# Local transformer inside a twelve-stage network: where the closing part's norm, its last products and the norm's result stand in a four-round schedule

## The chip, the core and the metric

The kernel runs on one core of one Trainium2 chip. The time is device microseconds of that core for one execution of the whole network. Of three runs of the kernel before, the median is 5578.49 us (5568.84 to 5580.77). One more execution was profiled; all views below come from it.

## The reference, cut to what matters

The network has twelve stages, each added to the running `x`. Two of them (seventh and ninth) are the same local transformer, six layers deep:

```python
for i in range(DEPTH):                       # DEPTH = 6
    x = attn_layer(shift_tokens(x), Wqkv[i], q_scale[i], k_scale[i], Wo[i]) + x
    x = ffn_layer(shift_tokens(x), ln_g[i], ln_b[i], W1[i], b1[i], W2[i], b2[i]) + x

def ffn_layer(x, g, bln, W1, b1, W2, b2):
    mu = x.mean(-1, keepdims=True)
    var = ((x - mu) ** 2).mean(-1, keepdims=True)
    xn = (x - mu) / jnp.sqrt(var + 1e-05) * g + bln
    a, gate = jnp.split(xn @ W1 + b1, 2, -1)
    return a * jax.nn.gelu(gate, approximate=False) @ W2 + b2
```

`attn_layer` has 16 heads of 64: projections, an l2 norm of q and k, a rotation of both, softmax over windows of 32 queries by 64 keys, weighted values, and the product with `Wo`. Everything is float32.

## The kernel before, in words

Features lie on the partitions, tokens along the free dimension. The 2048 tokens are four groups of 512. In a local stage, one layer of one group is a *unit*: 24 units per stage, 48 in the whole program. A unit's 16 heads are done four at a time, as four *quads*, so a stage has 96 quads.

`ffn2` (L1593) is a software pipeline written out by hand. Each pass of its loop is a *round*, in which four quads of different age are served: q0 is projected, q1 gets its scores, q2 its exponentials, transposes and weighted values, q3 its context turned back. The order of statements is the order in which each engine gets its work: `_Ordered` (L285) chains every engine's instructions, so none of the engines reorders them. In a steady round TensorE (PE) does this, with the tiles' names as the profile shows them: `bank<-sb_cs,l_rn` (quad_pick, L1361: 16 tiny matmuls; its start is used below as the start of a round), `pp` (quad_project, for k and then for q), `et` (quad_turn: transposes of the exponentials), `bank<-l_sq` (quad_norms), `ct` (quad_back), `cx` (quad_weigh: 128 small matmuls of 64x32 weights, in two halves of 64), `sc` (quad_scores: a mask, then 128 small matmuls), `vp` (quad_values). ScalarE (ACT) squares `pp` into `l_sq`, takes the exponential `l_e`, copies `et` out as `l_at` (which `cx` reads) and `ct` out as `l_ct`, does two steps for the roots (`lv`, `l_rn`) and copies `vp` out as `l_v`. VectorE (DVE) does `l_rq`, two shuffles, the scaled keys `l_kp`, then the start of the rotation (`l_yk`, a shuffle `l_yr`, `l_yq`, a second shuffle `l_yr`), then `l_rc` and `l_cx` for each half of `cx`, then `l_mx` and `l_e` from `sc`. GpSimd (POOL) finishes the rotation in four operations and scales `l_e`.

The large PSUM tiles (`pp`, `et`, `ct`, both halves of `cx`, `sc`, `vp`, `ge`) share three pairs of banks (`two`, L1294). Which pair each of them gets is settled when the program is built, so a reordering can give other instructions each other's buffers. Two more banks hold `bank` and `acc`.

The rest of a unit, its closing part, is the generator `local_rest` (L1472). `ffn2` advances it by one step at four places of each round: A after the q projection and before the transposes (L1620), B after the weighted values and before the scores (L1632), C right behind B (L1633), D after the values (L1638). So it runs over four rounds, sixteen places:

- first round, *output round*: three groups of products with `Wo` (`wo_acc`) at A, B and D; at D also x1 (the residual add) and its shifted copy.
- second, *norm round*: at A the norm's mean (a matmul with a constant matrix, in the profile `acc<-l_xs`), `ln_c` = x minus mean on DVE, its square `ln_sq` on ACT; nothing at B and C; at D the variance (`acc<-ln_sq`), Ln and Exp on ACT (`lv`, `ln_r`), and on DVE the result `t` = `ln_c` times `ln_r`, and then times gamma plus beta.
- third, *gelu round*: at C two of three `ge` pairs (products with W1, Gelu on ACT, `l_ag` on DVE), with a table load on ACT ahead; at D the third pair, a table load back, and the first two products with W2 (`second(0)` and `second(1)`, in the profile `w_acc`).
- fourth, *last round*: at A the third product and x2 (the residual add).

Where a step yields False at B or D, a piece of a background queue (the next stage's norms) is pumped; a step that yields True keeps it away. `settle` (L482) lets an unfinished background piece run to its end first, because the norm's working tiles (`scratch`, L405) are shared with it.

Of the kernel before, what the change touches and what calls it, by code (L numbers as in the profile page):

```python
# [23 lines left out]
AF = mybir.ActivationFunctionType  # L24
ALU = mybir.AluOpType
# [14 lines left out]
INNER = 341  # L40
# [268 lines left out]
class _Net:  # L309
# [1162 lines left out]
    def local_rest(self, u):  # L1472


        nc, i = self.nc, u.i
        acc = self.bank1("wo_acc")

        def project(cs):
            for c in cs:
                self.mm(acc, u.w["wo"][:, c, :], u.ct[c // 2][:, c % 2, :], start=c == 0, stop=c == 7)  # L1480

        project(range(3))
        yield False
        project(range(3, 6))
        yield False
        yield False
        project(range(6, 8))
        u.x1 = self.new_x()
        nc.vector.tensor_tensor(u.x1, acc, self.ys[u.g], ALU.add)
        xs = self.shifted(u.x1)  # L1490
        yield False

        self.settle()
        norm = self.norm_parts(xs, gamma=self.get(f"F{i}_ln_g"), beta=self.get(f"F{i}_ln_b"),
                               out=self.scratch("t", bufs=2), bank=self.bank1)
        next(norm)
        yield True
        yield True
        yield True
        u.hn = yield from norm  # L1500
        yield False

        yield False
        yield False
        o = self.bank1("w2_acc")
        ags = []

        def second(m):
            f = GE_CHUNKS[m][1]
            self.mm(o, u.w["w2"][:f, m, :], ags[m][:f, :], start=m == 0, stop=m == 2)  # L1510

        def first(m):
            f, w = GE_CHUNKS[m]
            pp = self.two("ge")
            self.mm(pp[:w, 0, :], u.w["w1"][:, INNER + f : INNER + f + w], u.hn)
            self.mm(pp[:w, 1, :], u.w["w1"][:, f : f + w], u.hn)
            gl = self.work("l_gl", bufs=2)
            self.act(gl[:w, :], pp[:w, 0, :], AF.Gelu, bias=self.get(f"F{i}_b1", 3 + m, 1)[:w, :])
            ag = self.work("l_ag", bufs=2)
            nc.vector.scalar_tensor_tensor(ag[:w, :], pp[:w, 1, :],  # L1520
                                           self.get(f"F{i}_b1", m, 1)[:w, :], gl[:w, :],
                                           ALU.add, ALU.mult)
            ags.append(ag)

        self.table("gelu_and_others")
        first(0)
        first(1)
        yield True
        first(2)
        self.table(LN_EXP)  # L1530
        second(0)
        second(1)
        yield False

        second(2)
        x2 = self.new_x()
        nc.vector.scalar_tensor_tensor(x2, o, self.get(f"F{i}_b2"), u.x1, ALU.add, ALU.add)
        self.ys[u.g] = x2
        if i == DEPTH - 1:
            z = self.new_x()  # L1540
            nc.vector.scalar_tensor_tensor(z, x2, 0.5, self.x[u.g], ALU.mult, ALU.add)
            self.finish(u.g, z)
        yield False
# [235 lines left out]
```

## Time and profile before

| what | value |
|---|---|
| median of three runs | 5578.49 us |
| the profiled execution | 5561.13 us, span 5559.4 us |
| PE busy | 5031.0 us (90%) |
| DVE, ACT, POOL busy | 3494.9, 2440.1, 2344.1 us |
| mean granted TensorE clock | 0.962 |
| norm matmuls, first to last start | 1089.5 to 4882.2 us |
| matmuls of the scores, first to last start | 985.3 to 4859.1 us |

Between the two local stages, from about 2800 to 3050 us, another stage runs. In the four views of the prediction's sample unit, times are microseconds from the start of the span. A timeline row gives start, duration, engine, operation, output<-inputs, count, and in brackets the idle time of the engine just before it with what ended it; "issue" there means that no semaphore did. L300 is the line of a recording helper and says nothing. Matmul ends are modelled, so distances from start to start are safer than durations.

### The profile page before, as it was taken

How to read it: one execution, taken by the hardware profiler on the slowest of the kernel's cores; microseconds unless marked ns; L12 is line 12 of the kernel's file. 1: busy time of each engine (PE TensorE's matmuls, PEld its weight loads, DVE VectorE, ACT ScalarE, POOL GpSimd, SP SyncE). 2: the span in 40 equal slices, each digit the busy share in tenths (PEclk: the TensorE clock that was granted, in tenths of full speed). 3: DMA queues.
4: the chain of work that ended last, by engine and by line, in shares of the span. 5: the costliest groups of instructions: out<-in, count | busy, mean ns of one | idle time of the engine just before them, and what ended most of it. 6: DMA issues, size and time to landing. Idle time of an engine off the chain costs nothing.

```text
span 5559.4 us, 161655 instructions
## 1 busy us (share of the span) xinstructions
PE 5031.0 (90%) x73456; PEld 3009.9 (54%) x73456; DVE 3494.9 (63%) x5863; ACT 2440.1 (44%) x2947; POOL 2344.1 (42%) x1205
## 2 busy tenths in 40 slices
PE   9999997899899899988889899989998988899889
PEld 6755754455555555555544455555555555555446
DVE  4444446767767767776645676767767676645555
ACT  2233235444545444444434444545444444433442
POOL 0000022666666666666500666666666666501000
PEclk9999999999999999999989999999999999999999
DMA  1000000111111111111000011111111111000000
GB/s 67 1 1 1 1 1 23 30 35 39 35 40 33 39 34 42 34 35 34 26 23 1 27 38 37 36 40 33 39 34 42 34 35 35 27 34 1 1 1 8
DMA packets 58334, 149.55 MB, mean 27 GB/s; under 512 B 9649, under 2 KB 23858, under 8 KB 57394
## 3 DMA queue, kind: packets, MB, share of 16 engines
q1 hardware_dynamic: 57650, 139.21, 8.3%
q8 instruction: 578, 9.47, 0.7%
q14 instruction: 106, 0.87, 0.1%
HBM read 45.52 MB, written 1.05 MB: 8 GB/s over the span
## 4 chain that ended last, share of the span: by engine, by line
PE 72%; DVE 17%; ACT 6%; issue 4%; POOL 1%; DMA 0%; SPq 0%; DVEq 0%; ACTq 0%; POOLq 0%
PE mm L355 10%; PE pp L300 10%; PE sc L300 7%; PE vp L300 7%; PE e_o L355 6%; PE wo_acc L300 6%; PE bank L300 6%; PE ge L300 5%; DVE l_yr L300 5%; PE cx L300 4%; PE ms L300 3%; PE w_acc L300 2%; DVE l_yk L300 2%; DVE l_yq L300 2%; PE ct L300 2%
## 5 line engine op out<-in xcount | busy, mean ns | idle before, releaser
L300 POOL TENSOR_TENSOR l_yr<-l_yr,l_ksin 128x1024 f32<-128x1024 f32 x192 | 456.8, 2379 | 1024.0 <-DVE l_yr L300 1024.0
L300 PE MATMUL pp<-l_xs,wqkv 128*128 128x512 f32 x1536 | 718.6, 611 | 5.3 <-DMA wqkv<-in_f_wqkv 3.7
L300 ACT COPY l_v<-vp 128x1024 f32<-128x1024 f32 x192 | 194.4, 1013 | 859.3 <-PE vp L300 859.3
L300 ACT ACTIVATE l_sq<-pp 128x1024 f32<-128x1024 f32 x384 | 391.4, 1019 | 283.3 <-PE pp L300 283.3
L300 DVE STREAM_SHUFFLE l_yr<-pp 128x1024 f32<-128x1024 f32 x384 | 505.9, 1318 | 0.0
L300 POOL TENSOR_TENSOR l_e<-l_e,l_rq 128x1024 f32<-128x1024 f32 x192 | 365.7, 1905 | 331.1 <-DVE l_e L300 301.4
L355 PE MATMUL mm<-x,m 128*128 128x512 f32 x1024 | 475.4, 604 | 1.4 <-ACT e_a L387 1.4
L300 DVE TENSOR_REDUCE l_mx<-sc 128x16 f32<-128x1024 f32 x192 | 235.1, 1224 | 374.6 <-PE sc L300 374.6
L300 POOL TENSOR_TENSOR l_yq<-l_yq,l_yr 128x1024 f32<-128x1024 f32 x192 | 456.0, 2375 | 15.0
L300 POOL TENSOR_TENSOR l_yk<-l_yk,l_yr 128x1024 f32<-128x1024 f32 x192 | 453.1, 2360 | 15.1
L300 POOL TENSOR_TENSOR l_yr<-l_yr,l_qsin 128x1024 f32<-128x1024 f32 x192 | 455.1, 2370 | 0.0
L300 PE MATMUL cx<-l_w,l_at 64*32 64x65 f32 x12288 | 304.0, 235 | 148.7 <-ACT l_at L300 123.2
L300 PEld LDWEIGHTS pp<-l_xs,wqkv 128*128 128x128 f32 x1536 | 279.1, 192 | 291.6 <-issue 285.8
L300 PE MATMUL sc<-l_kp,l_yq 64*32 64x64 f32 x24576 | 326.2, 236 | 104.1 <-issue 103.2
L300 PE MATMUL vp<-wqkv,l_xs 128*128 128x256 f32 x1536 | 399.5, 404 | 6.5 <-issue 5.3
L355 PEld LDWEIGHTS e_o<-m,e_h 128*128 128x128 f32 x3072 | 362.9, 192 | 60.6 <-issue 60.1
L300 PEld LDWEIGHTS sc<-l_kp,l_yq 64*32 64x32 f32 x24576 | 277.5, 111 | 172.0 <-issue 170.8
L300 PEld LDWEIGHTS cx<-l_w,l_at 64*32 64x32 f32 x12288 | 261.5, 109 | 197.7 <-ACT l_at L300 137.5
L355 PE MATMUL e_o<-m,e_h 128*128 128x128 f32 x3072 | 363.5, 275 | 0.0
L300 PE MATMUL wo_acc<-l_ct,wo 128*128 128x512 f32 x768 | 358.0, 599 | 0.1
L300 PEld LDWEIGHTS vp<-wqkv,l_xs 128*128 128x128 f32 x1536 | 286.3, 196 | 61.0 <-issue 10.5
L300 PE MATMUL cx<-l_v,l_at 64*32 64x65 f32 x12288 | 309.3, 236 | 6.0 <-issue 6.0
(285 smaller groups left out, 9513.1 us busy)
## 6 DMA issues: line engine op xcount, KB each, us to landing
l_w<-l_v SPq DMA_DIRECT2D x192, 390.0 KB
wqkv<-in_f_wqkv SPq DMA_DIRECT2D x48, 384.0 KB
l_w<-l_v SPq DMA_DIRECT2D x192, 65.0 KB
wo<-in_f_wo SPq DMA_DIRECT2D x12, 512.0 KB
l_rt<-l_rn SPq DMA_DIRECT2D x384, 8.0 KB
m<-in_m_w SPq DMA_DIRECT2D x16, 256.0 KB
w<-in_f_w SPq DMA_DIRECT2D x12, 341.0 KB
w<-in_f_w SPq DMA_DIRECT2D x12, 192.0 KB
```

The lines of the kernel that those rows point to most:

```text
L300: r = f(*args, **kw)
L355: self.nc.tensor.matmul(out, lhsT=lhsT, rhs=rhs, start=start, stop=stop)
```

## The change

Only `local_rest` changes, and all of it is a matter of place. The mean, `l_lc` (formerly `ln_c`) and the square move from A to B of the norm round. The variance, Ln and Exp stay at D. The two DVE operations that make the norm's result move from D of the norm round to A of the gelu round. `second(1)` moves from D of the gelu round, and `second(2)` with x2 from A of the last round, both to B of the last round. The centred x and the reciprocal root get tiles of their own (`l_lc`, `l_lr`). The places that pump the background queue are the same as before.

```diff
         xs = self.shifted(u.x1)
         yield False
 
+        yield False
         self.settle()
-        norm = self.norm_parts(xs, gamma=self.get(f"F{i}_ln_g"), beta=self.get(f"F{i}_ln_b"),
-                               out=self.scratch("t", bufs=2), bank=self.bank1)
-        next(norm)
+        xc, r = self.work("l_lc"), self.work("l_lr")
+        m = self.bank1("mean")
+        self.mm(m, self.get("mean"), xs)
+        nc.vector.tensor_tensor(xc, xs, m, ALU.subtract)
+        sq = self.scratch("ln_sq")
+        nc.scalar.activation(sq, xc, AF.Square)
         yield True
         yield True
-        yield True
-        u.hn = yield from norm
+        v = self.bank1("var")
+        self.mm(v, self.get("mean"), sq)
+        self.rsqrt(r, v, 0)
         yield False
 
+        hn = self.scratch("t", bufs=2)
+        nc.vector.tensor_tensor(hn, xc, r, ALU.mult)
+        nc.vector.tensor_scalar(hn, hn, self.get(f"F{i}_ln_g"), self.get(f"F{i}_ln_b"), ALU.mult,
+                                ALU.add)
         yield False
         yield False
         o = self.bank1("w2_acc")
...
         first(2)
         self.table(LN_EXP)
         second(0)
+        yield False
+
+        yield False
         second(1)
-        yield False
-
         second(2)
         x2 = self.new_x()
         nc.vector.scalar_tensor_tensor(x2, o, self.get(f"F{i}_b2"), u.x1, ALU.add, ALU.add)
```

In the built program the PSUM pairs of three of the four rounds are dealt out differently: in the norm round and the last round the second half of `cx` takes the pair of `ct` and so waits for ACT's `l_ct`; in the gelu round it takes the pair of the q projection and waits for DVE's second `l_yr`.

More of the change, by code (lines that the diff above doesn't have):

```diff
@@ L1514, in first @@
             pp = self.two("ge")
-            self.mm(pp[:w, 0, :], u.w["w1"][:, INNER + f : INNER + f + w], u.hn)
-            self.mm(pp[:w, 1, :], u.w["w1"][:, f : f + w], u.hn)
+            self.mm(pp[:w, 0, :], u.w["w1"][:, INNER + f : INNER + f + w], hn)
+            self.mm(pp[:w, 1, :], u.w["w1"][:, f : f + w], hn)
             gl = self.work("l_gl", bufs=2)
```

## The prediction

> **What bounds the kernel.** First the page's engine shares, then the longest waits of PE.
>
> ```profile
> PE 5031.0 (90%) x73456; PEld 3009.9 (54%) x73456; DVE 3494.9 (63%) x5863; ACT 2440.1 (44%) x2947; POOL 2344.1 (42%) x1205
> ```
>
> ```profile
> PE cx L300 <- ACT l_at L300: 123.2, 48, 3.3
> PE sc L300 <- issue: 103.2, 87, 2.0
> ...
> PE ge L300 <- DVE l_yr L300: 27.1, 43, 0.9
> ```
>
> PE is the bound; whatever shortens its queue in a round shortens the round. Of its idle time in the local stages, two entries stand out, and each comes about once per unit: 48 waits of `cx` for `l_at` (there are 48 units), and 87 waits of `sc` for nothing that has a semaphore. To place them I took one unit and asked for its norm, gelu and last rounds (they start at 1463.54, 1481.84 and 1503.03; the next round starts at 1517.81). On PE:
>
> ```profile
> 1474.17 0.25 PE L300 MATMUL cx<-l_w,l_at 64*32 64x65 f32 x2 [2.62 <-ACT l_at L300]
> ...
> 1478.04 1.09 PE L300 MATMUL sc<-l_kp,l_yq 64*32 64x64 f32 x88 [1.47 <-issue]
> ...
> 1486.45 1.09 PE L300 MATMUL et<-sb_c,l_e 128*128 128x128 f32 x8 [0.34 <-ACT l_e L300]
> ...
> 1492.31 3.70 PE L300 MATMUL ge<-t,w 128*128 128x512 f32 x8 [0.60 <-DVE l_yr L300]
> ...
> 1514.75 1.20 PE L300 MATMUL sc<-l_kp,l_yq 64*32 64x64 f32 x100 [1.59 <-issue]
> ```
>
> The first wait is the norm round's. Why `l_at` is late stands in ACT's queue:
>
> ```profile
> 1472.59 0.63 ACT L300 ACTIVATE ln_sq<-ln_c 128x512 f32<-128x512 f32 x1 [3.45 <-DVE ln_c L300]
> 1473.12 0.99 ACT L300 COPY l_at<-et 128x1024 f32<-128x1024 f32 x1
> ```
>
> ACT sat 3.45 us at the head of its queue for `ln_c`, which DVE reaches only behind the whole rotation; the copy that `cx` needs was queued behind it. The gelu round starts with DVE in the same position:
>
> ```profile
> 1483.39 0.85 DVE L300 TENSOR_TENSOR t<-ln_c,ln_r 128x512 f32<-128x512 f32 x1 [1.74 <-ACT ln_r L300]
> 1484.28 0.55 DVE L300 TENSOR_SCALAR t<-t,sb_pv 128x512 f32<-128x512 f32 x1
> 1484.74 0.17 DVE L300 TENSOR_SCALAR l_rq<-bank 128x16 f32<-128x16 f32 x1
> ```
>
> DVE waits 1.74 us for `ln_r` with keys and rotation behind it, so `l_rq` is done 3.1 us into the round, against 0.9 in the last round, and `cx` and `ge` are held by `l_yr`. The stretch from one round's start to the next, averaged over the trace: 19.0 us for 46 norm rounds, 21.4 for 44 gelu rounds, 15.3 for 44 last rounds (14.8 typical; four carry background work). Drains hold the others.
>
> **Dense work.** From start to start in rounds without a wait, PE needs: pick 0.57, `pp` 3.54, `et` 0.97, sums 0.99, `ct` 1.03, `cx` 1.42, mask 0.32, `sc` 1.41, `vp` 1.93; together 12.2 us. One 512-column float32 product of the closing part adds 0.86.
>
> **The stall in sc.** The last round holds one product: 12.2 + 0.86 = 13.05, against 14.8 measured, so the stall costs about 1.8 us, more than the 1.59 in the bracket (modelled ends). It comes in norm and last rounds, where `sc` follows `cx` directly; in output and gelu rounds 2.8 or 3.7 us of long matmuls lie between the two and `sc` shows none. Its place moves by some 25 matmuls from unit to unit. The page's queue 8, "instruction", moved 9.47 MB in 578 packets, 16.4 KB each. I read it as code arriving too slowly for 256 small matmuls in a row: 9.47 MB for PE's 146,912 instructions is 64 bytes each, so a block of 16 KB is 128 matmuls with their weight loads, run in 1.45 us, while 1.45 + 1.8 = 3.25 us (an estimate) passes between blocks. The Trainium skill speaks against this: "Runtime: NRT & Kernel Launch", section "Instruction fetch mechanics", gives the 16 KiB blocks of 256 instructions but says that fetching is mostly hidden, since issue is slower than the fill. By that rule a filler between `cx` and `sc` buys nothing; by the row it buys its own length, up to 1.8. I take the row, for the stall is absent just where filler stands, and keep the rule as a rival.
>
> **Norm round.** Removed: the mean ahead of `et`, `ln_sq` ahead of `l_at`. Without filler, `et` waits for the exponential and starts 4.6 into the round (gelu round's row) instead of 4.1 + 0.86. `ct` starts at 6.6, the first half of `cx` at 7.6; `l_at` is ready by then (gelu round: 6.75). The second half now waits for `l_ct`, which ended 2.15 us after `ct` began in the gelu round: 8.8 instead of 8.3, a new wait of 0.45. Its price lies between 0 and the 2.62 of the old wait; I take 0.45 because ACT has nothing ahead of `l_ct` now. `cx` ends at 9.5, the mean takes it to 10.4. The stall of 1.8 is covered by 0.86 and, half the time, by the 0.45: 0.7 is left. `sc` with mask 1.73 + 0.7 gives 12.8, `vp` 14.7, variance 15.6. Against 19.0: 3.4 us less. The old figure includes some 0.6 us of half-speed clock: the granted clock falls to 0.5 in 34 of the 46 norm rounds, behind the idle `cx`.
>
> Free moves: `l_lc` on DVE stands behind `l_cx`, ahead of `l_mx`, where DVE idled 2.33 us for `sc`; `ln_sq` falls into ACT's 4.71 us of idleness before `l_v`. Were that cover gone, each would cost its 0.65 us. Neither SP nor POOL is passed: shifted copy and all DMAs keep their places.
>
> **Gelu round.** Removed: 1.74 us of waiting and 1.4 of work ahead of `l_rq`. DVE then runs as in the last round, where the second `l_yr` ends at 8.67. The norm's result follows, 0.85 + 0.55: done at 10.1. Behind it are queued `l_rc` and `l_cx` (`ge` and the next `ct` wait for them; done 11.75 against 12.05 before) and the first `ge`, which begins at 10.1 instead of 10.66. `cx` is not in the way: its second half waits for `l_yr` to 8.7 and ends at 9.4. From `ge` on 3.63 + 0.32 + 1.42 + 1.83 + 1.72 as before, and one product instead of two, 0.9: 19.95. Bounds for `ge`: 9.4 (`cx`'s end) to 11.9 (no earlier rotation). Gain 1.45.
>
> **Last round.** `et` 4.6; `cx` as in the norm round, to 9.5; two products 1.72 in place of the one ahead of `et`; the stall covered; `sc` 1.73 and `vp` 1.93: 14.9. Before, 14.8 typical: nothing, for the stall pays for the product from the gelu round and the two waits. x2 (0.73) on DVE sits ahead of `l_mx` while PE is still in `sc`. `acc` is held until x2, at about 12, and next needed 7 us later. Bounds 14.4 to 16.7 (stall unchanged).
>
> **Output round.** No change; its exponential needs POOL's `l_e`, which ended 2.97 into it, 0.5 ahead of need. After: rotation 6.3 + 4 x 2.37, then 1.9, less 14.9: 2.8.
>
> **Sum.** 46 x 3.4 = 156, 44 x 1.45 = 64, 44 x 0.1 = -4: 216 us. The profiled execution took 5561.1 (span 5559.4 and 1.7 around it): 5345. It lies 17.4 below the median of the runs; the median should go to 5578.5 - 216 = 5362.
>
> **Rivals.** (1) The stall is no matter of filler and keeps its 1.8. Norm rounds gain 2.3 (106), gelu rounds 64, last rounds lose 1.9 (82): 88 less, 5490. For it: the skill's rule, and a single 0.86 product is short. Against: the two kinds of rounds without the stall. (2) The norm's result holds `ge` up: at 11.9 instead of 10.1 the gelu round loses 1.8, 79 in all: 5441. For it: `ge` is now right behind it. Against: the last round shows DVE 1.8 us earlier once nothing stands in front. (3) Slower: dealing the PSUM pairs differently makes a new standing wait. The second half of `cx` waits for `l_ct` or `l_yr` in norm, gelu and last rounds, 134 times. Above 216 / 134 = 1.6 us more each than I counted, the whole is slower; if all were as late as `l_at` was, 2.62, that is 2.17 more, 291 us: 5653. Against: `l_ct` took no longer than 2.15 us after `ct` in a round with a free ACT.
>
> **Numbers.** The forecast has 0.60, (1) or a part of it 0.20, (2) 0.14, (3) 0.04, and 0.02 for gains that cancel. 0.2% is 11 us, about what a measurement of this kernel can tell from no change. The range leaves out (3), the full (1), and, at the other end, gains above 270 (stall gone in the norm round too, `ge` at 9.4): 5305 to 5465.
>
> **What would show it.** `cx` no longer waits for `l_at`; instead a few tenths for `l_ct`. `sc` waits for issue in norm rounds only, under 1 us, and not in last rounds. `ge` starts near 10.1 and waits for `t`. Half-speed clock spells become rare. Norm round 15.6, gelu 19.95, last 14.9. The forecast is wrong if last rounds grow past 16, or if norm rounds stay above 17.

## The result, and the profile after

The kernel after takes 5530.21 us (median of 4 runs, 5525.49 to 5541.67), the kernel before beside it 5573.66 (4 runs, 5567.54 to 5580.77): a ratio of 0.9928, interval 0.9908 to 0.9949. So the change gains 43 us where 216 were forecast. The sign was right, a fifth of the size was there.

The page's engine shares after. The same work is done, yet DVE is busy for 3609 us instead of 3495, and no operation was added to it (5863 instructions both times):

```profile
PE 5082.7 (92%) x73456; PEld 2989.8 (54%) x73456; DVE 3609.2 (65%) x5863; ACT 2447.6 (44%) x2947; POOL 2365.2 (43%) x1205
```

The longest waits of PE after (total us, times, longest):

```profile
PE et L300 <- ACT l_e L300: 78.0, 146, 7.2
PE ge L300 <- DVE l_rc L300: 73.6, 32, 2.6
...
PE ge L300 <- DVE t L300: 39.7, 12, 3.8
PE cx L300 <- ACT l_ct L300: 31.1, 100, 0.3
...
PE sc L300 <- issue: 20.8, 31, 1.6
```

Both old waits went as forecast: `cx` for `l_at` (123.2 us) has left the list, and `sc` for issue fell from 103.2 to 20.8. The small new wait of `cx` for `l_ct` came too, 0.31 each where 0.45 was reckoned. What the forecast did not have is the wait of `ge`: 112.2 us in the 44 gelu rounds, one wait in each, against 27.1 before. (The two `ge` lines above also hold two waits outside these rounds, and two of the rounds' waits stand under issue.)

The kinds of rounds show what came of each part. Mean time from one round's start to the next, worked out from the start times in each trace (46 output, 46 norm, 44 gelu, 44 last rounds; ten more at the ends of the stages are of no kind), with the start of the first `ge` within the gelu round:

| kernel | output | norm | gelu | last | first `ge` at |
|---|---|---|---|---|---|
| before | 19.75 | 19.00 | 21.39 | 15.29 | 10.66 |
| forecast | 19.75 | 15.6 | 19.95 | 15.4 | 10.1 |
| after | 19.59 | 15.85 | 23.08 | 15.86 | 12.13 |

Norm rounds gained 145 us in all. Gelu rounds, which were to gain 64, lost 75; last rounds lost 25, output rounds gained 7: 53 us gained. Against that, the ten other rounds take 6 us more, and the two drains (what follows the last round of a local stage) 16 more. The profiled execution after also enters the local stages 11 us later, in stages that the change doesn't touch; ahead of them its trace has 109 us of half clock, that of before 89. That leaves 20 us, and the two spans differ by 19.5. (The profiled execution after, 5541.67 us, is the slowest of its four.)

The prediction's sample unit has its gelu round at 1482.20 now. DVE's rows (start, duration, engine, operation):

```profile
1489.33 1.34 DVE L300 STREAM_SHUFFLE l_yr<-pp 128x1024 f32<-128x1024 f32 x1
1490.57 0.78 DVE L300 TENSOR_TENSOR t<-l_lc,l_lr 128x512 f32<-128x512 f32 x1
1491.38 2.45 DVE L300 TENSOR_SCALAR t<-t,sb_pv 128x512 f32<-128x512 f32 x1
1493.75 0.20 DVE L300 RECIPROCAL l_rc<-cx 128x8 f32<-128x8 f32 x1
```

The second `l_yr` ends 8.47 into the round, earlier than the 8.67 forecast. But the operation that takes gamma and beta, 0.55 in the row of before, has 2.45. It is the same instruction on a tile of the same size, and it shows no wait: its own duration is longer. POOL's rows of the same time:

```profile
1488.39 2.40 POOL L300 TENSOR_TENSOR l_yr<-l_yr,l_ksin 128x1024 f32<-128x1024 f32 x1 [4.00 <-DVE l_yr L300]
1490.87 2.67 POOL L300 TENSOR_TENSOR l_yk<-l_yk,l_yr 128x1024 f32<-128x1024 f32 x1
1493.51 2.52 POOL L300 TENSOR_TENSOR l_yr<-l_yr,l_qsin 128x1024 f32<-128x1024 f32 x1
```

The slow operation is issued while POOL is in `l_yk`, and ends at 1493.83, 0.29 after it. And `l_yk`, 2.36 elsewhere, takes 2.67: it began while DVE's product ran, and that ended 0.48 later. In all 44 gelu rounds the slow operation starts 0.50 to 0.51 us behind the start of `l_yk`, ends 0.28 to 0.29 behind its end, and takes 2.44 us or more. The other four of its 48 runs lie in the drains, where POOL runs nothing beside them, and take 0.546. In before, POOL stood idle at the time of this operation (`l_e` ended at 1483.70, the operation ran at 1484.28, POOL's next began at 1489.97). On PE, the row of the first two `ge` pairs, and the granted clock (`PEclk`) around it:

```profile
1493.97 5.37 PE L300 MATMUL ge<-t,w 128*128 128x512 f32 x8 [2.38 <-DVE l_rc L300]
```

```profile
core 0: us, PE busy (x) PEld busy (x) DVE busy (x) ACT busy (x) POOL busy (x), PEclk, DMA share, GB/s
1489.00:1491.60 2.60, 2.57 (x136) 2.08 (x135) 2.56 (x5) 1.61 (x3) 2.52 (x2) 1.00 0.00 0
1491.60:1494.00 2.40, 0.03 (x1) 0.06 (x1) 2.37 (x3) 2.00 (x2) 2.40 (x2) 1.00 0.04 10
1494.00:1496.00 2.00, 2.00 (x4) 0.77 (x5) 1.48 (x3) 0.00 (x0) 2.00 (x1) 0.67 0.01 4
1496.00:1498.00 2.00, 2.00 (x4) 0.96 (x3) 0.19 (x1) 0.69 (x1) 1.92 (x2) 0.50 0.00 0
1498.00:1499.40 1.40, 1.40 (x5) 0.33 (x4) 0.56 (x1) 0.02 (x1) 0.46 (x1) 0.97 0.00 0
```

PE is idle for 2.38 us, and then runs its large matmuls at half the clock for 3.4 us (two thirds of the first 2 us, all of the next 2, little of the rest): the eight take 5.37 us instead of 3.70. The bracket names `l_rc`, the operation behind the slow one, which ends 0.02 before `ge` starts and whose data `ge` does not read; `t` ended at 1493.83.

### The profile page after: what moved, and what is told of

Read it like the earlier page. It is cut to its first block, busy times and chain, and to the rows that moved or that the text cites. A ratio compares the mean times of both kernels' runs of the same rounds, so it can differ in the third digit from the quotient of the medians.

```text
span 5539.9 us, 161681 instructions
## 1 busy us (share of the span) xinstructions
PE 5082.7 (92%) x73456; PEld 2989.8 (54%) x73456; DVE 3609.2 (65%) x5863; ACT 2447.6 (44%) x2947; POOL 2365.2 (43%) x1205
## 4 chain that ended last, share of the span: by engine, by line
PE 76%; DVE 12%; ACT 8%; issue 3%; POOL 1%; DMA 0%; SPq 0%; DVEq 0%; ACTq 0%; POOLq 0%
PE pp L300 10%; PE mm L355 10%; PE bank L300 7%; PE e_o L355 6%; PE sc L300 6%; PE vp L300 6%; PE wo_acc L300 6%; PE ge L300 6%; PE cx L300 3%; PE et L300 3%; PE ct L300 3%; PE ms L300 3%; DVE t L300 2%; ACT l_sq L300 2%; PE w_acc L300 2%
## 5 line engine op out<-in xcount | busy, mean ns | idle before, releaser
L300 POOL TENSOR_TENSOR l_yk<-l_yk,l_yr 128x1024 f32<-128x1024 f32 x192 | 467.5, 2435 | 15.1
L300 PE MATMUL ge<-t,w 128*128 128x512 f32 (+1 forms) x576 | 321.2, 703 | 117.9 <-DVE l_rc L300 73.6
L300 PE MATMUL vp<-wqkv,l_xs 128*128 128x256 f32 x1536 | 383.6, 392 | 3.6 <-issue 1.4
L300 PE MATMUL sc<-l_kp,l_yq 64*32 64x64 f32 x24576 | 302.2, 225 | 21.5 <-issue 20.8
```

The costliest lines, as they stand in the source:

```text
L300: r = f(*args, **kw)
```

## The experiments

The theory, called theory A in the expectations: the gamma-and-beta operation is held on DVE for as long as the POOL operation beside it runs, `ge` starts late by that much, and the idle PE gets a lower clock on top. The rivals: `ge` waits for a PSUM pair that was dealt out anew, or for `l_rc` (theory B); whatever DVE does between the rotation and `l_rc` comes too late at this place, whoever runs beside it (theory C); or another of the three moves spoils the gelu rounds. All kernels were timed against the kernel before on their own chip. Round means of all of them stand in one table behind the runs.

### The held operation

**no_scale** drops the operation; everything else stays.

```diff
         nc.vector.tensor_tensor(hn, xc, r, ALU.mult)
-        nc.vector.tensor_scalar(hn, hn, self.get(f"F{i}_ln_g"), self.get(f"F{i}_ln_b"), ALU.mult,
-                                ALU.add)
```

> The changed kernel with the second operation of the norm's result (times gamma plus beta, on DVE) left out, 48 times; everything else in place. Theory A (that operation is held until POOL's running operation ends: 2.45 us in place of 0.55, and PE, idle for it, falls to half clock): ge starts near 9.5 us into the gelu round instead of 12.1, the four ge matmuls take 3.7 again instead of 4.8, the gelu round is about 19.5 instead of 23.1, the whole about 5530 - 44 x 3.6 = 5370 us. Theory B (the new deal of the PSUM pairs or l_rc holds ge): only the work of 0.55 us goes, about 5500 us. Theory C (anything that DVE does between the rotation and l_rc is too late there): the product alone still holds ge; about 5450 us.

Measured: 5375.44 us, 0.966 of before (0.9643 to 0.9676). One instruction of 0.55 us, 48 times (26 us at its old price), is worth some 149 us between this kernel and the kernel after (from the two ratios). The gelu round falls from 23.08 to 19.62, `ge` starts at 9.74, and its first group takes 3.71 instead of 4.79 us. A new PSUM pair is hardly what held `ge`: TensorE's order of work is that of the kernel after, and its other rounds kept their times.

**pool_quiet** leaves DVE alone and takes POOL's operations away from beside it.

```diff
-        nc.gpsimd.tensor_tensor(four(yr), four(yr), q.tab[n + "sin"], ALU.mult)
-        nc.gpsimd.tensor_tensor(y, y, yr, ALU.add)
+        quiet = q.n % 4 == 0 and q.n >= 8
+        if not (quiet and n == "q"):
+            nc.gpsimd.tensor_tensor(four(yr), four(yr), q.tab[n + "sin"], ALU.mult)
+        if not quiet:
+            nc.gpsimd.tensor_tensor(y, y, yr, ALU.add)
```

> The changed kernel, in which POOL leaves out, in gelu rounds alone, the last three of the four operations of the rotation (k's add, q's product with the sine, q's add), so that POOL is idle from 8.6 us on; DVE's list of work is that of the changed kernel. Theory A: times gamma plus beta takes 0.55 us again, ge starts at 10.1 to 10.3, gelu round about 20.1, the whole about 5530 - 44 x 3 = 5400 us. Theories B and C: nothing on DVE or PE is changed, so the operation and the round stay at 2.45 and 23 us, the whole at 5530 us.

Measured: 5397.61 us, 0.9698 (0.9679 to 0.9717). This is the run that names POOL. The row of the operation in before, after and pool_quiet (count, then minimum/median/maximum in ns, first and last start); one of the 49 belongs to another stage:

```profile
L300 DVE TENSOR_SCALAR t<-t,sb_pv x49: 545/546/548, 296.7 to 4888.4; 128x512 f32<-128x512 f32 x49
```

```profile
L300 DVE TENSOR_SCALAR t<-t,sb_pv x49: 545/2452/2457, 308.4 to 4867.5; 128x512 f32<-128x512 f32 x49
```

```profile
L300 DVE TENSOR_SCALAR t<-t,sb_pv x49: 545/546/548, 300.7 to 4725.8; 128x512 f32<-128x512 f32 x49
```

Same instruction, same place in DVE's queue, same product ahead of it: without POOL beside it, it is back at 0.546 us. That it is slow in this place by itself is excluded, and so is a PSUM pair, for the list of work of TensorE and of DVE is that of the kernel after.

**two_inputs** asks whether another form of the operation would escape: beta, one column, is read as a second tile operand from SBUF.

```diff
-        nc.vector.tensor_scalar(hn, hn, self.get(f"F{i}_ln_g"), self.get(f"F{i}_ln_b"), ALU.mult,
-                                ALU.add)
+        nc.vector.scalar_tensor_tensor(hn, hn, self.get(f"F{i}_ln_g"),
+                                       self.get(f"F{i}_ln_b").to_broadcast([P, T]), ALU.mult,
+                                       ALU.add)
```

> The changed kernel, with times gamma plus beta in the same place on DVE, but as an operation of two inputs from SBUF (beta read as a broadcast second operand) instead of one; alone such an operation takes about 0.7 us. If only the short form with one input is held by a running POOL operation: 0.7 to 0.8 us, ge near 10.3, the whole about 5405 us (ratio 0.972). If one with two SBUF inputs is held as well: about 2.5 us as in the changed kernel, the whole about 5525 us (0.993).

Measured: 5545.89 us, 0.9976 (0.9967 to 0.9985), gelu rounds of 23.29. It is held as well:

```profile
L300 DVE SCALAR_TENSOR_TENSOR t<-t,sb_pv x48: 751/2716/2725, 1108.1 to 4850.8; 128x512 f32<-128x512 f32 x48
```

### The same work elsewhere

**result_back** puts both operations of the result back to D of the norm round; mean and products stay moved. Its edit takes the `yield False` from between the root and the product and puts it behind the result.

> The changed kernel with both operations of the norm's result put back behind Ln and Exp at D of the norm round; mean, square and the W2 products stay at their new places. Theory A: the second operation meets no running POOL operation there and takes 0.55 again, the gelu round is that of the kernel before less one product, about 20.5; norm and last rounds stay near 15.8 and 15.3; the whole about 5530 - 44 x 2.6 = 5415 us. Theory B: the PSUM pairs are dealt as in the changed kernel, the gelu round stays over 22.5 and the whole within 5500 to 5540 us.

Measured: 5425.51 us, 0.9751 (0.9732 to 0.9771): some 98 us better than the kernel after (from the two ratios), which has the result behind the rotation. The operation takes 0.546 there, the product ahead of it 0.69 to 1.91 us. But `l_rq` and the rotation wait for the root again, `ge` starts at 10.89, and the gelu round takes 20.77.

**scale_on_act** leaves the product behind the rotation and gives gamma and beta to ACT at B, as the scale and bias of an Identity.

```diff
-        nc.vector.tensor_scalar(hn, hn, self.get(f"F{i}_ln_g"), self.get(f"F{i}_ln_b"), ALU.mult,
-                                ALU.add)
         yield False
+        self.act(hn, hn, AF.Identity, scale=self.get(f"F{i}_ln_g"), bias=self.get(f"F{i}_ln_b"))
```

> The changed kernel with times gamma plus beta done by ACT at B of the gelu round, behind l_rn and ahead of the table load, instead of by DVE at A. Theory A: no operation of this kind is left on DVE; ACT is done near 10.8 us into the round, ge starts there, no fall of the clock; gelu round about 20.9, the whole about 5530 - 44 x 2.2 = 5433 us. Theory C (a result this late holds ge whatever engine makes it): ge near 12, about 5530 us.

Measured: 5442.33 us, 0.978 (0.9762 to 0.9798). ACT takes 0.80 us for it (0.797 to 0.815), so it is not held there, but it comes after the product and ACT's other work: `ge` starts at 11.06, 1.5 us of it waited, and the gelu round takes 21.08.

### Each part alone

Each of these starts from the kernel before and makes one of the three moves. **mean_only** moves the mean, `l_lc` and the square from A to B. **result_only** moves the two operations of the result from D of the norm round to A of the gelu round. **products_only** moves the products:

```diff
         second(0)
+        yield False
+
+        yield False
         second(1)
-        yield False
-
         second(2)
```

> The kernel before, with mean, l_lc and square alone moved to B of the norm round; the result stays at D of it, the products where they were. If the copy queued behind the square was the whole of the norm round's wait, the norm round is 15.8 instead of 19.0 and nothing else moves: about 5565 - 46 x 3.1 = 5420 us (ratio 0.974). If the other two moves are needed for it: over 5480 us.

> The kernel before, with the two operations of the norm's result alone moved to A of the gelu round (own tiles for both inputs); mean and square stay at A of the norm round, the products where they were. If the held operation is the whole cause, this move alone costs: ge at about 12.1 us instead of 10.7 and four ge matmuls partly at half clock, the gelu round about 24 instead of 21.4, the whole about 5565 + 44 x 2.6 = 5680 us (ratio 1.02). By the prediction's arithmetic (0.55 for that operation) it gains 0.5 us a round: 5540 us.

> The kernel before, with second(1), second(2) and x2 alone moved to B of the last round. If the wait of sc without a semaphore is slow code and a filler between cx and sc covers it: no such wait in last rounds, last round about 15.2 instead of 14.8 typical, gelu round shorter by one product (0.9), together 0.5 us a unit: about 5540 us (ratio 0.996). If filler doesn't cover it: last round about 16.7, the whole about 5565 + 44 x 0.9 = 5605 us.

Measured: mean_only 5425.16 us, 0.9753 (0.9738 to 0.9768). result_only 5686.97 us, 1.0224 (1.0208 to 1.024). products_only 5557.21 us, 0.9992 (0.9982 to 1.0002). On that chip the kernel before took 5561.6, so the three are worth -137, +124 and -4 us (from the ratios). The whole gain is the mean's; the result's move gives most of it back; the products' move is worth nothing that can be told. They add to -17, the whole made -40 (from its own ratio). The gelu rounds show a difference of that size: the parts' changes there add to +2.22 us a round, together they made +1.69, and 44 times 0.53 is 23. Each ratio's interval is some 6 to 11 us to either side, so more than this can't be read from the 23.

In result_only the operation stands at the same 2.45 us with nothing else moved:

```profile
L300 DVE TENSOR_SCALAR t<-t,sb_pv x49: 545/2453/2462, 300.5 to 5005.9; 128x512 f32<-128x512 f32 x49
```

The waits of PE in mean_only and in products_only show where the products' gain went:

```profile
PE sc L300 <- issue: 65.6, 66, 1.8
PE et L300 <- ACT l_e L300: 56.2, 101, 5.7
```

```profile
PE cx L300 <- ACT l_at L300: 123.3, 48, 3.3
PE et L300 <- ACT l_e L300: 52.7, 99, 6.0
...
PE sc L300 <- issue: 43.7, 54, 1.9
...
PE cx L300 <- ACT l_ct L300: 16.8, 59, 0.3
```

With the products between `cx` and `sc`, the stall of `sc` is down from 103.2 to 43.7 us. But `et` has lost the product that stood ahead of it, and waits for `l_e` in the last round now; the second half of `cx` waits for `l_ct`; and one product more is in the round. Last rounds went from 15.29 to 15.86, gelu rounds from 21.39 to 20.57: 25 us lost, 36 won. The drains lose 12 more: from the start of the last round to the second local stage, and behind that stage to the end of the span, it is 319.0 and 719.0 us, against 312.4 and 713.4 in before. In mean_only (310.6 and 712.5) and result_only (312.4 and 712.2) they have not grown, so most of the 16 us by which the kernel after lost there belongs to the products' move. The measured ratio leaves no more than 10 us of gain.

### Two versions that avoid the operation

**fold_beta** computes the whole reference without it. Gamma goes into the product, and beta goes through W1 into the bias, once per layer: six products with one column in an output round, and two small additions.

```diff
+        if u.g == 0:
+            bp = self.spare()[:, :6]
+            for k in range(2):
+                for m, (f, w) in enumerate(GE_CHUNKS):
+                    self.mm(bp[:w, 3 * k + m : 3 * k + m + 1],
+                            u.w["w1"][:, INNER * k + f : INNER * k + f + w],
+                            self.get(f"F{i}_ln_b"))
...
-        nc.vector.tensor_tensor(hn, xc, r, ALU.mult)
-        nc.vector.tensor_scalar(hn, hn, self.get(f"F{i}_ln_g"), self.get(f"F{i}_ln_b"), ALU.mult,
-                                ALU.add)
+        nc.vector.scalar_tensor_tensor(hn, xc, self.get(f"F{i}_ln_g"), r, ALU.mult, ALU.mult)
...
-            self.act(gl[:w, :], pp[:w, 0, :], AF.Gelu, bias=self.get(f"F{i}_b1", 3 + m, 1)[:w, :])
+            self.act(gl[:w, :], pp[:w, 0, :], AF.Gelu, bias=u.w["b1"][:w, 3 + m : 4 + m])
```

**fold_prod_back** is the same with the products at their old places.

> The changed kernel, with the second operation of the result done away with: gamma goes into the product (one DVE operation, x minus mean times gamma times root), and beta is brought in once per layer and stage by six one-column matmuls of W1 with beta, added to b1 on the chip (12 times, some 2 us each). Computes the whole reference. Theory A: the gelu round is that of the run without this operation, 19.6, the whole 5375 + 12 x 2 = about 5400 us (ratio 0.970). If the product with two SBUF inputs is held too when POOL is running, ge would be near 10.5 and the whole about 5430 us.

> The run with beta folded into b1, with the W2 products back at their old places. The run with the products alone moved was level with the kernel before, so this should be level with the folded run: about 5393 us (ratio 0.969), last round 14.8 and gelu round 20.1 in place of 15.2 and 19.2 typical. If the products' place does matter in the faster kernel: 15 us or more off.

Measured: fold_beta 5393.5 us, 0.9693 (0.9679 to 0.9707); fold_prod_back 5387.5 us, 0.9693 (0.9679 to 0.9708). Both beat the kernel after by 2.4% by these ratios, and they cannot be told apart: once more the products are worth nothing. The remaining operation has two inputs in SBUF and lies in the same place, yet it isn't held. fold_beta's rows of DVE and POOL, in a gelu round near the sample's time, show why:

```profile
1470.60 0.75 DVE L300 SCALAR_TENSOR_TENSOR t<-l_lc,sb_pv,l_lr 128x512 f32<-128x512 f32 x1
```

```profile
1468.42 2.38 POOL L300 TENSOR_TENSOR l_yr<-l_yr,l_ksin 128x1024 f32<-128x1024 f32 x1 [3.99 <-DVE l_yr L300]
1470.88 2.69 POOL L300 TENSOR_TENSOR l_yk<-l_yk,l_yr 128x1024 f32<-128x1024 f32 x1
```

It starts 0.28 us ahead of POOL's `l_yk`, and 0.27 to 0.31 ahead in all 44 gelu rounds. Here DVE is first and POOL pays, 2.69 us instead of 2.36; the second operation of the kernel after came 0.5 us behind the start of `l_yk`, and DVE paid. POOL's `l_yr` is by its record still running for 0.2 us when the operation starts, and this costs it next to nothing (0.758 us, median, where the two-input form of two_inputs takes 0.75 in the drains); why the last 0.2 us of a record hold nobody is not shown.

All rounds together (means, us; the last column is how long the first `ge` group of four matmuls took):

| kernel | output | norm | gelu | last | `ge` at | `ge` took |
|---|---|---|---|---|---|---|
| before | 19.75 | 19.00 | 21.39 | 15.29 | 10.66 | 3.70 |
| after | 19.59 | 15.85 | 23.08 | 15.86 | 12.13 | 4.79 |
| no_scale | 19.54 | 15.84 | 19.62 | 15.82 | 9.74 | 3.71 |
| pool_quiet | 19.52 | 15.83 | 20.29 | 15.84 | 10.25 | 3.87 |
| two_inputs | 19.57 | 15.86 | 23.29 | 15.77 | 12.39 | 4.73 |
| result_back | 19.59 | 15.83 | 20.77 | 15.80 | 10.89 | 3.72 |
| scale_on_act | 19.55 | 15.82 | 21.08 | 15.87 | 11.06 | 3.85 |
| mean_only | 19.66 | 15.89 | 21.63 | 15.26 | 10.87 | 3.74 |
| result_only | 19.70 | 18.82 | 24.19 | 15.29 | 12.02 | 5.15 |
| products_only | 19.65 | 18.92 | 20.57 | 15.86 | 10.67 | 3.74 |
| fold_beta | 19.93 | 15.82 | 19.65 | 15.79 | 9.78 | 3.70 |
| fold_prod_back | 19.98 | 15.80 | 20.45 | 15.27 | 9.73 | 3.70 |

## Why the prediction was right and wrong

**The norm round was right.** 15.85 us against 15.6 forecast, 145 us against 156. `cx` no longer waits for `l_at`, and mean_only shows that this move alone makes 0.9753. That the whole came out faster at all hangs on this term: the mean's 137 us are little more than the 124 that the result's move loses.

**The stall in sc was right as a place, worth little as a gain.** It gave way to what stands between `cx` and `sc`: last rounds have 0.09 us of it on average where before had 1.20, norm rounds 0.18 where it had 0.97. Rival 1 falls: 82 us of stall were bought off. That it is code, as the prediction read it against the rule that it cites, the trace of before bears out: in its DMA records each of the 80 stalls of `sc` over 0.5 us ends 1.2 to 1.6 us after a packet of queue 8 ("instruction") has landed, while the stall's place in the run of `sc` varies by 2.5 us, and the starts of matmuls of `sc` in output and gelu rounds lie anywhere from 0 to 5 us behind such a landing. No run changed how the code comes. In the last round the stall that was bought off paid for what came in, about as the forecast said (typical round 15.2 against 14.9, mean 0.57 above before, where 0.1 was forecast): the two products took 1.92 us (median), not 1.72, and `et` and `cx` wait a little each.

**The step that failed** is in the gelu round: "The norm's result follows, 0.85 + 0.55: done at 10.1." The start was right (8.37 into the round); the product took 0.78, the second operation 2.45, so it was done at 11.63 in the sample, and `ge` started at 12.13 on average. The term 0.55 was a row of before, measured with POOL idle, and it was carried to a place at which POOL runs four operations of 2.36 us in a row. Of POOL the prediction asked whether its own queue is passed ("Neither SP nor POOL is passed") and when it is done, and it put POOL's effect on DVE at nothing; yet its own line "rotation 6.3 + 4 x 2.37" has POOL busy from 6.3 to 15.8 us into a round, and so all through 8.7 to 10.1. The hold alone is 1.90 of the 2.03 us by which `ge` was late, and pool_quiet, which takes POOL away, brings `ge` forward by 1.88. The forecast took no clock cost from it: the first `ge` group takes 4.79 instead of the 3.63 forecast, 1.16 us more. Together 3.19 us, and the gelu round is 3.13 above its forecast: 44 times that is 138 us. Between the two profiled executions 196 of the 216 us are missing (173 between the medians): these 138, the last rounds' 21, the norm rounds' 11, 16 in the drains, 6 in the ten other rounds and the 11 us of the late entry, less 7 of the output rounds.

The upper bound for `ge`, 11.9, was set by a late rotation, and lay under what came. Rival 2 had the place (the norm's result holds `ge` up) and a time of 5441, with the wrong reason: the rotation did come 1.8 us earlier. Rival 3, new waits for PSUM pairs, had the mechanism in the trace, at 0.31 us a wait.

**What could have been read.** Whoever moves an operation to another time has to ask what runs on the other engines at that time, and not only on its own. The trace of before held signs of it. An operation of another norm, of 0.69 us as a rule, has one run of 2.89:

```profile
L300 DVE TENSOR_TENSOR x<-ln_c,ln_r x24: 691/692/2887, 313.1 to 5357.6; 128x512 f32<-128x512 f32 x24
```

It began at 977.26, just when POOL had begun an `l_yr` of 2.35 us (977.25). And in the sample unit's output round, DVE's `l_kp`, 1.23 us as a rule, took 1.68 while POOL was in `l_e` (until 1445.86):

```profile
1445.27 1.68 DVE L300 SCALAR_TENSOR_TENSOR l_kp<-l_sq,l_yk 128x1024 f32<-128x1024 f32 x1
```

```profile
1443.96 1.90 POOL L300 TENSOR_TENSOR l_e<-l_e,l_rq 128x1024 f32<-128x1024 f32 x1
```

And the Trainium skill, "SBUF — State Buffer", section "Who interferes with whom", says it: VectorE and GpSimd share a pair of ports into SBUF under an exclusive lock, which the instruction issued first keeps to its end while the other stands still; a tensor_scalar can take that pair, and an operation with two inputs in SBUF contends with one of GpSimd that reads. The runs agree in each point that they can show: 2.45 us for the tensor_scalar and 2.72 for the form with two inputs behind POOL's start, 0.55 and 0.75 without POOL, 2.69 for POOL behind DVE's start. That a port is what they share is the page's word; the runs show that one stands still. As an estimate from this rule and the rows of before, the term was up to 0.55 plus one POOL operation, 2.36, which is 2.91, and the bound for `ge` 10.1 + 2.36 = 12.5.

The clock was the second half. Behind PE's idle time ahead of `ge` came spells of half clock in 29 of the 44 gelu rounds after, 102 us in all; in these rounds the first `ge` group took 5.37 us on average, in the other 15 it took 3.67, though in 14 of those PE had waited 2.37 us or more as well. What decides between the two is not shown. Before, the same had happened in 34 of the 46 norm rounds, behind the late `l_at` (160 us). The forecast had such spells become rare; in large part they moved to another kind of round: in the 190 rounds together there are 195 us at half clock before, 116 after, 44 in mean_only, 17 in fold_beta and 311 in result_only. (Some 220 to 270 us more lie outside the rounds in each of them.)

**What stays open.** Why the products' move makes the drains longer was not tried. Nor was a form of the operation with one SBUF input that does not take the shared pair, if there is one for this arithmetic.

## What to carry to other kernels

Price a moved operation by what runs beside it at the new place: on VectorE, look at what GpSimd does there, and move the operation to where GpSimd is idle, start it first, or fold it into another. A hold of this kind shows in no list of waits: compare the operation's own minimum and median duration, and overlay the two engines. When a gain is far smaller than the work freed, split the change into its parts: here one part had it all, one gave most of it back, and one was worth nothing.

## What the runs showed of the hardware

An operation of VectorE that is held is recorded as long and not as waiting: 0.546 became 2.45 us behind a GpSimd operation of 2.36, and the operation queued behind it is named as the releaser. It works both ways, 2.36 to 2.69 for GpSimd where VectorE was first. Behind an idle stretch of TensorE of 2.4 us came 3.4 us or more of half clock in 29 of 44 gelu rounds, which cost 1.1 us per gelu round on average; the Trainium skill, "TensorE: Matmul & The Clock Gate", section "Why this matters for your kernels", warns of gaps above about 3 us, and these rounds show it from a shorter one, though not each time. With 1.9 us of long matmuls between two runs of 128 small ones, a stall for instructions that took 1.20 us per last round fell to 0.09; but the filler came from places where it had covered other waits, and bought nothing that could be measured.
